# Graph attention and mean aggregation from neighbour lists: another order of the work where the adjacency ends and layer 0 begins, and biases folded on VectorE

## The chip, the cores and the metric

One core of a Trainium2 chip runs the whole kernel in one launch. The metric is the time on the device in microseconds. The kernel before takes 719.69 us, the median of 3 runs (718.86 to 720.13). The profile is of one execution with a span of 718.4 us.

## The reference

x is 4096 x 512, adj a 4096 x 4096 matrix of 0 and 1 with about four ones in a row. Two layers, each a graph layer with a residual and a layer norm:

```python
# layer 0: 8 heads of 64 columns
Wh = einsum('nf,hfo->hno', x, W)
f1 = einsum('hno,ho->hn', Wh, a[:, :64]); f2 = einsum('hno,ho->hn', Wh, a[:, 64:])
e = leaky_relu(f1[:, :, None] + f2[:, None, :], 0.2)
attn = softmax(where(adj > 0, e, -9e15), axis=-1)
x = layernorm(x + heads_side_by_side(attn @ Wh))
# layer 1
mask = (adj > 0); deg = mask.sum(1)
agg = mask @ x / maximum(deg, 1)
out = concat([x @ W_self + b_self, agg @ W_nb + b_nb]) @ W_comb + b_comb
x = layernorm(x + relu(out))
```

## The kernel before, in words

**Lists instead of masks.** Since a row of adj has few ones, the kernel turns every row into a list of column numbers and then gathers rows of a table in memory. The rows are worked on in 32 blocks of 128. A list has 3 places of its own (K0) and, for longer rows, shared places in two columns (KH) that one-hot matrices ("own", "st") tie to their rows. What doesn't fit sets a flag, and a dense program (`dense_layers`) runs; it doesn't run here.

**Stage 1, the lists** (lines 712 to 821). The loop over b has 30 turns (LB = 30), and blocks 30 and 31 come after it. For each block two loads of 1 MB bring the adjacency (`load_adj`, tile "at", 4 buffers, on SyncE's queue). ScalarE turns each half into bf16 (`mask_adj`, tile "ab", 3 buffers). TensorE packs the bits into keys (`fold_adj`, L395) and VectorE takes the greatest keys (`max_keys`, L410). Beside it `node_block` (L319) makes the rows of table t0, Wh with f2 in front, and stores them. Every four blocks a `decode` turns keys into column numbers; it's a generator, and each `some(lists)` runs one piece of it up to the next `yield`.

**The joint** (lines 812 to 858). The node rows of blocks 30 and 31 are finished; blocks 30 and 31 of the adjacency are loaded, masked, folded and decoded; the gathers of layer 0 for blocks 0 and 1 start (L515, GpSimd, five instructions of 128 rows for a block), those of later blocks once the pool of the adjacency ("lists") is closed. `fold_weights` (L259, L270) multiplies W_nb by the lower half of W_comb into m2, in four quarters, also as a generator. `fold_bias` (L279 to L289) turns b_nb into a column and multiplies it by the same half of W_comb: four products with one row of result, added to brow by VectorE.

**Stage 2, layer 0** (lines 864 to 902). Turn i works on several blocks at once: the layer norm of block i (`a_moments`, L611; `root`; `norm`), the weighted sum of block i+1 (L583, L595, L605, L607), the weights of block i+2 (`a_weights`, L539), and the product of block i-1 with m2 (`a_z`, L632), which is stored into table t1. Turns 2 to 7 also run one piece each of the last decode, that of blocks 28 to 31.

**Stage 3** (lines 903 to 924): W_self is multiplied by the upper half of W_comb into m1, its bias likewise, and `spread_bias` (L295) copies the summed bias row to all 128 partitions with a product by a row of ones. **Stage 4, layer 1** (lines 941 to 964): gathers from t1 (again 160 instructions), own rows times m1 (L656), sums, layer norm, store.

**What sets the order.** The program runs under `manual_schedule`: each engine works in the order of the text. The waits between the engines follow from the tiles: a tile taken from a pool with n buffers waits until the tile n before it in that pool has been read for the last time. The "own" tiles (4 buffers) serve both `decode` of early blocks and `owners`; PSUM tiles "sm", "pw", "nm" have 2 buffers, "key" has 1.

Of the kernel before, what the change touches and what calls it, by code (L numbers as in the profile page):

```python
# [40 lines left out]
P = 128  # L41
# [14 lines left out]
G = 4  # L56
# [30 lines left out]
def listed_layers(  # L87
# [112 lines left out]
    nc.vector.memset(onec, 1.0)  # L200
    eps = const.tile([P, 1], F32, name="eps")
    nc.vector.memset(eps, EPS)
    oner = const.tile([1, P], F32, name="oner")
    nc.vector.memset(oner, 1.0)
    inv_n = const.tile([P, 1], F32, name="inv_n")
    nc.scalar.mul(inv_n, onec, 1.0 / N)

# [39 lines left out]
    def load_bias(k):  # L247
        brw = small.tile([FB, P], F32, name="brw", bufs=1)
        nc.scalar.dma_start(brw, (b_self, b_nb)[k].rearrange("(c p) -> c p", p=P))
        return brw  # L250

    def fold_weights(loaded, m, wp, tag):

        wr, wc = loaded

        def turned(c):
            tp = ps.tile([P, FB, P], F32, name="sm", bufs=2)
            for d in range(FB):
                nc.tensor.transpose(tp[:, d, :], wr[:, c, ts(d, P)], ident)  # L259
            wT = wp.tile([P, FB, P], F32, name="xT", bufs=2)  # L260
            nc.scalar.copy(wT, tp)
            return wT

        wT = turned(0)
        for c in range(FB):
            nxt = turned(c + 1) if c + 1 < FB else None
            yield
            mp = ps.tile([P, HD], F32, name=tag, bufs=2)
            for d in range(FB):
                nc.tensor.matmul(  # L270
                    mp, lhsT=wT[:, d, :], rhs=wc[:, d, :], start=(d == 0), stop=(d == FB - 1)
                )
            nc.scalar.copy(m[:, c, :], mp)
            wT = nxt

    def fold_bias(loaded, brw):

        bt = ps.tile([P, FB], F32, name="sm", bufs=2)
        nc.tensor.transpose(bt, brw, ident[0:FB, 0:FB])  # L279
        bcol = small.tile([P, FB], F32, name="bcol", bufs=1)  # L280
        nc.scalar.copy(bcol, bt)
        yield
        bp = ps.tile([1, HD], F32, name="sm", bufs=2)
        for d in range(FB):
            nc.tensor.matmul(
                bp, lhsT=bcol[:, d : d + 1], rhs=loaded[1][:, d, :],
                start=(d == 0), stop=(d == FB - 1),
            )
        nc.vector.tensor_add(brow[0:1, :], bp, brow[0:1, :])  # L289
        yield  # L290

    def spread_bias():

        bp = ps.tile([P, HD], F32, name="sm", bufs=2)
        nc.tensor.matmul(bp, lhsT=oner, rhs=brow[0:1, :], start=True, stop=True)  # L295
        nc.scalar.copy(brow, bp)


# [64 lines left out]

    loads, masks, keys, kks = {}, {}, {}, {}

    def load_adj(b, ap, hs=range(NH)):

        for h in hs:
            at = loads[b, h] = ap.tile([P, NG // NH, SC], I32, name="at", bufs=4)
            r = b * P + h * (P // NH)  # L370
            nc.sync.dma_start(
                at, adj[r : r + P // NH, :].rearrange("(j r) (s c) -> (r s) j c", r=RG, s=SEG)
            )

    def mask_adj(b, h, ap):
        ab = masks[b, h] = ap.tile([P, NG // NH, SC], BF16, name="ab", bufs=3)
        nc.scalar.activation(  # L377
            ab, loads.pop((b, h)), AF.Relu, accum_out=asum[:, b, h : h + 1]
        )
# [32 lines left out]
    def decode(b0, dp, place, slow=False):  # L412
# [22 lines left out]
        for g in range(G):  # L435
            nc.vector.max(nb[:, g, 0:8], kj[:, g, :])
            nc.vector.match_replace(kj[:, g, :], nb[:, g, 0:8], kj[:, g, :], 0.0)
            nc.vector.max(nb[:, g, 8:16], kj[:, g, :])
        yield
        va = dp.tile([P, G, KL], F32, name="va", bufs=1)  # L440
        nc.vector.tensor_scalar(va, nb, float(SHIFT), None, OP.is_ge)
        nc.vector.tensor_reduce(deg[:, bs], va, AX.X, OP.add)
# [83 lines left out]
    def a_owners(b, wp):  # L526
        OWN[b] = owners(b, wp)
# [159 lines left out]
    def some(todo):  # L687
        for p in todo:
            next(p, None)
# [30 lines left out]
    pa = []  # L720
    for k in range(2):
        pa.append(ps.tile([P, HD], F32, name=("sm", "key")[k], bufs=(2, 1)[k]))
        nc.tensor.matmul(pa[k], lhsT=oner, rhs=av[0:1, k], start=True, stop=True)
    nc.scalar.copy(av[:, 0], pa[0])
    xT = transposed(0, wp)
    prs = fp.tile([P, FB, HD], F32, name="wc")
# [44 lines left out]
    def store(w, row, eng=nc.scalar):  # L771
        eng.dma_start(t0[2 + w * P : 2 + (w + 1) * P, :], row[:, 0:TW])
# [5 lines left out]
    for b in range(LB):  # L778
        for k in range(1 + (b == AHEAD)):
            load_x(w + k + XL)  # L780
            sum_x(w + k + XL, xacc)
        if b + 2 < LB:
            load_adj(b + 2, ap)
        elif b + 2 == LB:
            loaded = load_fold(1, w_nb, fp)
            load_adj(LB, ap, (0,))
        if b == 3:
            brw = load_bias(1)
            nc.scalar.dma_start(brow[0:1, :], b_comb.rearrange("(a o) -> a o", a=1))
            pads(wp)  # L790
        some(lists)
        nxt = transposed(w + 1, wp)
        if w > 0:
            store(w - 1, row)
        if b + 1 < LB:
            key_bank(b + 1)
            for h in range(NH):
                mask_adj(b + 1, h, ap)
            row = node_block(w, xT, b)
            w, xT = w + 1, nxt  # L800
        if b == AHEAD:
            nxt = transposed(w + 1, wp)
            store(w - 1, row)
            row = node_block(w, xT)
            w, xT = w + 1, nxt
        if b == 24:
            pieces = mean_row(w_sb, xacc, wp)
        if b >= 24:
            next(pieces, None)
        if b % G == G - 1:  # L810
            lists = [*lists[-1:], decode(b + 1 - G, dp, on_own)]
    row = node_block(w, xT)
    store(w, row)
    fold_adj(LB - 1, dp)
    max_keys(LB - 1)
    row = node_block(w + 1, nxt)
    store(w + 1, row, nc.sync)
    load_adj(LB, ap, (1,))
    load_adj(LB + 1, ap)
    xa_cm.__exit__(None, None, None)  # L820

# [2 lines left out]
    for b in range(2):  # L824
        G0[b] = gather(t0, b, gps)
    m2s = fold_weights(loaded, m2, wp, "pw")
    next(m2s)
    mask_adj(LB, 0, ap)
    some(lists)
    next(m2s)  # L830
    key_bank(LB)
    mask_adj(LB, 1, ap)
    some(lists)
    next(m2s)
    some(lists)
    fold_adj(LB, dp)
    max_keys(LB)
    a_owners(0, wp)
    a_owned(0, wp)
    mask_adj(LB + 1, 0, ap)  # L840
    next(m2s)
    key_bank(LB + 1)
    mask_adj(LB + 1, 1, ap)
    fold_adj(LB + 1, dp)
    max_keys(LB + 1)
    ap_cm.__exit__(None, None, None)
    gps += [ctx.enter_context(tc.tile_pool(name=f"gat{k}", bufs=1)) for k in range(2, GA)]
    sp_cm = tc.tile_pool(name="last", bufs=1, side="right")
    sp = sp_cm.__enter__()
    lists = [decode(NB - G, dp, on_last, slow=True)]  # L850
    some(lists)
    next(m2s, None)
    some(lists)
    for _ in fold_bias(loaded, brw):
        pass
    some(lists)
    m1_pool = ctx.enter_context(tc.tile_pool(name="m1", bufs=1))
    m1 = m1_pool.tile([P, FB, HD], F32, name="m1")
# [2 lines left out]
    def on(b):  # L861
        return 0 <= b < NB

    for i in range(-2, NB + 2):
# [5 lines left out]
            xT = transposed(i - 1, wp)  # L870
        if on(i + 1):
            a_reach(i + 1)
        if i >= -1 and on(i + 2):
            a_owned(i + 2, wp)
        if on(i + 1):
# [6 lines left out]
            root(i, xs[:, i, :])  # L882
        if on(i + 2):
            a_exp(i + 2)
        if on(i):
            norm(i, xs[:, i, :])
        if on(i - 1):
# [10 lines left out]
        if i == 1:  # L898
            loaded = load_fold(0, w_self, fp)
            brw = load_bias(0)  # L900
        if 2 <= i < 8:
            some(lists)
    for _ in fold_weights(loaded, m1, wp, "nm"):
        pass
    for _ in fold_bias(loaded, brw):
        pass
    spread_bias()


    sp_cm.__exit__(None, None, None)  # L910
# [446 lines left out]
```

## Time and profile before

| what | from the profile |
|---|---|
| span | 718.4 us, 9039 instructions |
| TensorE products, weight loads | 646.3 us (90%), 365.2 us (51%) |
| VectorE, ScalarE, GpSimd | 488.8 (68%), 443.7 (62%), 360.5 us (50%) |
| memory | 165.29 MB read, 25.31 MB written, 265 GB/s over the span |
| gathers L515 | 320, 951 ns each |
| masks L377 | 64, 1911 ns each |
| products of the weight fold L270 | 64 passes, 3.70 us for a quarter of 8 |

The page cuts the span into 40 slices and gives a digit for each engine, the busy share in tenths. They show that no engine sets the pace throughout, so a share of the whole span says little: one reads the stage that a change touches. In the time line each row is a group of like instructions of one engine with its start, length and, in brackets, the idle time of the engine before it and what ended that. L numbers are lines of the kernel before.

### The profile page before, as it was taken

The numbers are of one execution on the slowest core, as the hardware profiler recorded it, in microseconds if no ns is written. First come the engines' busy times: TensorE is split into PE (matmuls) and PEld (weight loads), VectorE is DVE, ScalarE is ACT, GpSimd is POOL, SyncE is SP. The second block draws the span as 40 slices with busy tenths as digits, with TensorE's granted clock in tenths as the row PEclk, the third lists the DMA queues.
The fourth block names the chain that finished last, engine by engine and source line by source line (L and its number), as shares of the span: only waits on it lengthen the run. The fifth ranks groups of instructions, "written<-read, shape, count | busy, mean of one in ns | idle before, by whom it ended". The sixth has DMA issues, their size and how long they took to land. (4 is left out here: it accounts for less than half of the span.)

```text
span 718.4 us, 9039 instructions
## 1 busy us (share of the span) xinstructions
PE 646.3 (90%) x2534; PEld 365.2 (51%) x2534; DVE 488.8 (68%) x1424; ACT 443.7 (62%) x915; POOL 360.5 (50%) x403
## 2 busy tenths in 40 slices
PE   4797888887999769999999999999999999999992
PEld 2465666655676335555555555554344444444440
DVE  5266777875876378999999999981116665566553
ACT  3567777676784315556666576664237777677764
POOL 6512222121002476566666666400777777777770
PEclk9989999999999978999999999999989999999997
DMA  9999999999997676977877887611667888888883
GB/s 282 389 352 394 393 393 394 393 391 392 390 391 265 216 211 204 316 213 206 231 228 231 232 227 230 185 44 45 200 203 245 258 254 260 254 258 258 262 255 108
DMA packets 84263, 191.28 MB, mean 266 GB/s; under 512 B 12513, under 2 KB 12521, under 8 KB 84206
## 3 DMA queue, kind: packets, MB, share of 16 engines
q0 software_dynamic: 25600, 84.56, 40.2%
q1 hardware_dynamic: 53952, 97.53, 37.0%
q10 hardware_dynamic: 4654, 8.54, 3.1%
q8 instruction: 22, 0.36, 0.2%
q14 instruction: 35, 0.29, 0.1%
HBM read 165.29 MB, written 25.31 MB: 265 GB/s over the span
## 5 line engine op out<-in xcount | busy, mean ns | idle before, releaser
L515 POOL DMA_INDIRECT g<-t,idx x320 | 304.4, 951 | 172.4 <-issue 120.2
L377 ACT ACTIVATE ab<-at 128x2048 bf16<-128x2048 int32 x64 | 122.3, 1911 | 55.8 <-DMA at<-in_adj_dram 49.6
L319 PE MATMUL pw<-w_sb,xT 128*128 128x264 f32 x512 | 133.4, 407 | 1.0 <-DVE row L323 0.9
L632 PE MATMUL pw<-m,xT 128*128 128x512 f32 x256 | 118.0, 604 | 3.1 <-ACT xT L313 1.7
L319 PEld LDWEIGHTS pw<-w_sb,xT 128*128 128x128 f32 x512 | 96.4, 198 | 29.3 <-issue 4.7
L313 ACT COPY xT<-tp 128x512 f32<-128x512 f32 x80 | 46.3, 579 | 91.5 <-PE tp L311 89.8
L305 POOL TENSOR_TENSOR xacc<-xacc,xs 128x512 f32<-128x512 f32 x32 | 41.1, 1284 | 122.6 <-DMA xs<-in_x_dram 122.0
L583 DVE TENSOR_TENSOR g<-g,key 128x1024 f32<-128x1024 f32 x64 | 77.9, 1217 | 1.1
L632 PEld LDWEIGHTS pw<-m,xT 128*128 128x128 f32 x256 | 46.1, 190 | 55.3 <-issue 45.8
L595 PE MATMUL nm<-g,own 128*128 128x512 f32 x128 | 66.3, 643 | 0.0
L656 PE MATMUL nm<-m,xT 128*128 128x512 f32 x128 | 60.4, 617 | 1.3 <-ACT xT L313 1.3
L311 PEld LDWEIGHTS tp<-ident,xs 128*128 128x128 f32 x320 | 40.9, 148 | 36.1 <-issue 29.8
L656 PE MATMUL pw<-m,xT 128*128 128x512 f32 x128 | 57.6, 593 | 0.0
L311 PE MATMUL tp<-ident,xs 128*128 128x128 f32 x320 | 50.6, 283 | 6.0 <-DMA xs<-in_x_dram 5.8
L323 DVE COPY row<-pw 128x264 f32<-128x264 f32 x64 | 27.1, 425 | 33.3 <-PE pw L319 23.9
L656 PEld LDWEIGHTS nm<-m,xT 128*128 128x128 f32 x128 | 24.1, 199 | 26.1 <-issue 24.6
L670 DVE SCALAR_TENSOR_TENSOR sm<-y,lst,nm 128x512 f32<-128x512 f32 x16 | 12.1, 755 | 36.7 <-PE nm L663 36.6
L670 DVE SCALAR_TENSOR_TENSOR sm<-y,lst,pw 128x512 f32<-128x512 f32 x16 | 12.1, 755 | 34.3 <-PE pw L663 34.3
L656 PEld LDWEIGHTS pw<-m,xT 128*128 128x128 f32 x128 | 23.2, 191 | 23.4 <-issue 23.4
L663 PE MATMUL pw<-g,own 128*128 128x512 f32 x64 | 31.4, 615 | 3.0 <-DMA g<-t,idx 3.0
L595 PEld LDWEIGHTS nm<-g,own 128*128 128x128 f32 x128 | 23.1, 200 | 16.9 <-issue 16.1
L549 PEld LDWEIGHTS sm<-e,own 128*128 128x128 f32 x128 | 19.8, 199 | 22.7 <-ACT e L543 11.6
(178 smaller groups left out, 1031.1 us busy)
## 6 DMA issues: line engine op xcount, KB each, us to landing
at<-in_adj_dram SPq DMA_DIRECT2D x64, 1024.0 KB, 11.2
t<-row SPq DMA_DIRECT2D x32, 256.0 KB, 3.6
out_dram<-row SPq DMA_DIRECT2D x32, 256.0 KB, 3.8
t<-row ACTq DMA_DIRECT2D x31, 260.0 KB, 6.0
xs<-in_x_dram SPq DMA_DIRECT2D x31, 256.0 KB, 11.5
g<-t,idx POOLq DMA_INDIRECT x320, 4.1
wc<-in_L_gnn_W_comb_dram SPq DMA_DIRECT2D x2, 1024.0 KB, 14.8
w_sb<-in_L_gnn_W_dram SPq DMA_DIRECT2D x8, 128.0 KB, 4.4
```

The costliest lines, as they stand in the source:

```text
L305: nc.gpsimd.tensor_tensor(xacc, xacc, xs[:, b, :], OP.add)
L311: nc.tensor.transpose(tp[:, c, :], xs[:, b, ts(c, P)], ident)
L313: nc.scalar.copy(t, tp)
L319: nc.tensor.matmul(pw, lhsT=xT[:, c, :], rhs=w_sb[:, c, k * HW : (k + 1) * HW], start=(c == 0), stop=(c == FB - 1),)
L323: nc.vector.tensor_copy(row[:, k * HW : (k + 1) * HW], pw)
L377: nc.scalar.activation(ab, loads.pop((b, h)), AF.Relu, accum_out=asum[:, b, h : h + 1])
L515: nc.gpsimd.indirect_dma_start(out=g[:, k, 0 : table.shape[1]], out_offset=None, in_=table[:, :], in_offset=bass.IndirectOffsetOnAxis(ap=i ...
L583: nc.vector.tensor_tensor(gv if to is None else to.rearrange("p (k h d) -> p k h d", k=1, h=H), gv, E[b][:, sl].unsqueeze(3).to_broadcast( ...
L595: nc.tensor.matmul(NM[b], lhsT=OWN[b][:, k, :], rhs=G0[b][:, K0 + k, H:TW], start=False, stop=(k == KH - 1), skip_group_check=True,)
L632: nc.tensor.matmul(pz, lhsT=xT[:, c, :], rhs=m2[:, c, :], start=(c == 0), stop=(c == FB - 1))
L656: nc.tensor.matmul(NM[b], lhsT=xT[:, c, :], rhs=m1[:, c, :], start=False, stop=False, skip_group_check=True,)
L663: nc.tensor.matmul(NM[b], lhsT=OWN[b][:, k, :], rhs=g[:, K0 + k, 0:HD], start=False, stop=(k == KH - 1), skip_group_check=True,)
```

## The change

It does these things:

- Block 30's second adjacency half is loaded with the first, at b = 28; only block 31 is loaded at the joint. Both halves of block 30 are masked before the last node block, and block 30 is folded before the weight product begins.
- `fold_weights` has a second `yield` after each quarter's product, so that the copy of a quarter can stand later than its product. Its pieces are spread anew: three quarters before layer 0, the last in turn i = -1.
- `a_owners(0)` stands before the last piece of decode(24).
- The last decode (`slow`) takes its maxima in four pieces. One piece runs before layer 0, one in turn -2, the others in turns 2 to 11.
- Biases: the bias column is made by `bias_column` (at b = 5 for W_nb, after layer 0 for W_self). `fold_bias` now multiplies the rows of W_comb by that column on VectorE, four instructions that add into brow, which is 128 partitions of partial sums. `sum_bias` adds these over the partitions and spreads the sum with one product by a 128 x 128 tile of ones, which takes the place of the row of ones.

It is meant to bring the last adjacency work and the start of layer 0 forward, and to take the one-row products off TensorE.

```diff
     eps = const.tile([P, 1], F32, name="eps")
     nc.vector.memset(eps, EPS)
-    oner = const.tile([1, P], F32, name="oner")
-    nc.vector.memset(oner, 1.0)
+    ones = const.tile([P, P], F32, name="ones")
+    nc.vector.memset(ones, 1.0)
     inv_n = const.tile([P, 1], F32, name="inv_n")
     nc.scalar.mul(inv_n, onec, 1.0 / N)
...
                     mp, lhsT=wT[:, d, :], rhs=wc[:, d, :], start=(d == 0), stop=(d == FB - 1)
                 )
+            yield
             nc.scalar.copy(m[:, c, :], mp)
             wT = nxt
-    def fold_bias(loaded, brw):
+    def bias_column(k, brw):
         bt = ps.tile([P, FB], F32, name="sm", bufs=2)
         nc.tensor.transpose(bt, brw, ident[0:FB, 0:FB])
-        bcol = small.tile([P, FB], F32, name="bcol", bufs=1)
+        bcol = small.tile([P, FB], F32, name=f"bcol{k}", bufs=1)
         nc.scalar.copy(bcol, bt)
-        yield
-        bp = ps.tile([1, HD], F32, name="sm", bufs=2)
+        return bcol
+
+    def fold_bias(loaded, bcol):
+
         for d in range(FB):
-            nc.tensor.matmul(
-                bp, lhsT=bcol[:, d : d + 1], rhs=loaded[1][:, d, :],
-                start=(d == 0), stop=(d == FB - 1),
-            )
-        nc.vector.tensor_add(brow[0:1, :], bp, brow[0:1, :])
-        yield
-
-    def spread_bias():
+            nc.vector.scalar_tensor_tensor(
+                brow, loaded[1][:, d, :], bcol[:, d : d + 1], brow, OP.mult, OP.add
+            )
+
+    def sum_bias():
         bp = ps.tile([P, HD], F32, name="sm", bufs=2)
-        nc.tensor.matmul(bp, lhsT=oner, rhs=brow[0:1, :], start=True, stop=True)
+        nc.tensor.matmul(bp, lhsT=ones, rhs=brow, start=True, stop=True)
         nc.scalar.copy(brow, bp)
...
     loads, masks, keys, kks = {}, {}, {}, {}
-    def load_adj(b, ap, hs=range(NH)):
-
-        for h in hs:
+    def load_adj(b, ap):
+
+        for h in range(NH):
             at = loads[b, h] = ap.tile([P, NG // NH, SC], I32, name="at", bufs=4)
             r = b * P + h * (P // NH)
...
             nc.vector.match_replace(kj[:, g, :], nb[:, g, 0:8], kj[:, g, :], 0.0)
             nc.vector.max(nb[:, g, 8:16], kj[:, g, :])
-        yield
+            if slow or g == G - 1:
+                yield
         va = dp.tile([P, G, KL], F32, name="va", bufs=1)
         nc.vector.tensor_scalar(va, nb, float(SHIFT), None, OP.is_ge)
...
     for k in range(2):
         pa.append(ps.tile([P, HD], F32, name=("sm", "key")[k], bufs=(2, 1)[k]))
-        nc.tensor.matmul(pa[k], lhsT=oner, rhs=av[0:1, k], start=True, stop=True)
+        nc.tensor.matmul(pa[k], lhsT=ones[0:1, :], rhs=av[0:1, k], start=True, stop=True)
     nc.scalar.copy(av[:, 0], pa[0])
     xT = transposed(0, wp)
...
         elif b + 2 == LB:
             loaded = load_fold(1, w_nb, fp)
-            load_adj(LB, ap, (0,))
+            load_adj(LB, ap)
         if b == 3:
             brw = load_bias(1)
+            nc.vector.memset(brow, 0.0)
             nc.scalar.dma_start(brow[0:1, :], b_comb.rearrange("(a o) -> a o", a=1))
             pads(wp)
...
             row = node_block(w, xT)
             w, xT = w + 1, nxt
+        if b == 5:
+            bcol = bias_column(1, brw)
         if b == 24:
             pieces = mean_row(w_sb, xacc, wp)
...
     row = node_block(w, xT)
     store(w, row)
+    key_bank(LB)
+    for h in range(NH):
+        mask_adj(LB, h, ap)
     fold_adj(LB - 1, dp)
     max_keys(LB - 1)
     row = node_block(w + 1, nxt)
     store(w + 1, row, nc.sync)
-    load_adj(LB, ap, (1,))
     load_adj(LB + 1, ap)
     xa_cm.__exit__(None, None, None)
...
         G0[b] = gather(t0, b, gps)
     m2s = fold_weights(loaded, m2, wp, "pw")
-    next(m2s)
-    mask_adj(LB, 0, ap)
-    some(lists)
-    next(m2s)
-    key_bank(LB)
-    mask_adj(LB, 1, ap)
-    some(lists)
-    next(m2s)
     some(lists)
     fold_adj(LB, dp)
     max_keys(LB)
-    a_owners(0, wp)
-    a_owned(0, wp)
-    mask_adj(LB + 1, 0, ap)
     next(m2s)
     key_bank(LB + 1)
+    some(lists)
+    for k in range(3):
+        next(m2s)
+    mask_adj(LB + 1, 0, ap)
+    a_owners(0, wp)
+    fold_bias(loaded, bcol)
+    some(lists)
     mask_adj(LB + 1, 1, ap)
+    next(m2s)
     fold_adj(LB + 1, dp)
     max_keys(LB + 1)
+    a_owned(0, wp)
+    next(m2s)
     ap_cm.__exit__(None, None, None)
     gps += [ctx.enter_context(tc.tile_pool(name=f"gat{k}", bufs=1)) for k in range(2, GA)]
...
     sp = sp_cm.__enter__()
     lists = [decode(NB - G, dp, on_last, slow=True)]
-    some(lists)
-    next(m2s, None)
-    some(lists)
-    for _ in fold_bias(loaded, brw):
-        pass
     some(lists)
     m1_pool = ctx.enter_context(tc.tile_pool(name="m1", bufs=1))
...
         if on(i + 1):
             a_reach(i + 1)
+        if i == -1:
+            next(m2s)
         if i >= -1 and on(i + 2):
             a_owned(i + 2, wp)
...
         if on(i + 2):
             a_exp(i + 2)
+        if i == -2:
+            next(m2s)
+            some(lists)
         if on(i):
             norm(i, xs[:, i, :])
...
             loaded = load_fold(0, w_self, fp)
             brw = load_bias(0)
-        if 2 <= i < 8:
+        if i == -1:
+            next(m2s, None)
+        if 2 <= i < 12:
             some(lists)
+    bcol = bias_column(0, brw)
+    fold_bias(loaded, bcol)
     for _ in fold_weights(loaded, m1, wp, "nm"):
         pass
-    for _ in fold_bias(loaded, brw):
-        pass
-    spread_bias()
+    sum_bias()
```

## The prediction

> **What bounds the kernel now.** I read the busy digits of the page first, to cut the span into stages, then the groups, then the time line around the joint that the diff edits.
>
> ```profile
> POOL 6512222121002476566666666400777777777770
> PEclk9989999999999978999999999999989999999997
> ...
> L515 POOL DMA_INDIRECT g<-t,idx x320 | 304.4, 951 | 172.4 <-issue 120.2
> ```
>
> A slice is 17.96 us. To slice 12 the adjacency streams in; slices 12 to 14 are the joint; to slice 26 runs layer 0; from slice 28 layer 1. L515 is every row gather; 160 belong to each layer. Idle time of GpSimd between the layers is one stretch of 41.6 us. Busy times of stretches (PE, PEld, DVE, ACT, POOL, then clock, DMA share, GB/s):
>
> ```profile
> 225.30:257.00 31.70, 24.28 (x84) 10.71 (x84) 15.49 (x65) 13.05 (x20) 17.04 (x18) 0.95 0.71 239
> 257.00:282.60 25.60, 19.79 (x60) 11.51 (x61) 19.92 (x53) 9.18 (x26) 16.99 (x18) 0.67 0.68 195
> 282.60:329.20 46.60, 43.91 (x179) 24.64 (x177) 43.07 (x115) 27.87 (x73) 28.72 (x31) 1.00 0.83 259
> 501.90:700.00 198.10, 195.44 (x551) 91.66 (x550) 100.68 (x222) 126.07 (x306) 149.97 (x159) 0.98 0.79 245
> ```
>
> Layer 1: 159 gathers start in 198.1 us, 1.246 us apiece, 0.95 of instruction and 0.30 of issue. The first starts at 501.88, the last at 701.19; 159 steps of 1.25 us make 198.8 of these 199.3 us. So layer 1 is a fixed length from its first gather, which waits for the last z rows in t1. **What counts is only when layer 0 ends.**
>
> Layer 0: the moments instruction L611 of blocks 0, 1, 2, 3, 8, 11 and 31 starts at 266.72, 275.38, 282.60, 290.98, 329.23, 349.63 and 488.57. Without decode work a block takes 6.80 us, VectorE without a gap; later 6.93 to 6.98, TensorE as the close second. From 282.6 to 329.2 VectorE has no gap to speak of, and what its last decode adds is paid in full: 46.63 - 6 x 6.80 = 5.83 us. So the joint, 225 to 283, can be shortened, and VectorE work put into blocks 2 to 10 comes back. The joint, in the time line:
>
> ```profile
> 225.28 1.55 SPq L371 DMA_DIRECT2D at<-in_adj_dram  x3
> ...
> 235.27 0.61 PE L395 MATMUL key<-ab,fold 128*32 128x512 bf16 x8
> ...
> 238.52 5.12 PE L270 MATMUL pw<-wc,xT 128*128 128x512 f32 x8
> ...
> 244.68 1.91 ACT L377 ACTIVATE ab<-at 128x2048 bf16<-128x2048 int32 x1
> ...
> 246.73 0.61 PE L395 MATMUL nm<-ab,fold 128*32 128x512 bf16 x6 [1.53 <-ACT ab L377]
> ...
> 247.45 0.89 DVE L410 MAX8 kk<-nm 128x8 f32<-128x128 f32 x4 [9.29 <-PE nm L395]
> ...
> 255.34 0.68 DVE L289 TENSOR_TENSOR brow<-sm,brow 1x512 f32<-1x512 f32 x1 [0.60 <-PE sm L285]
> ...
> 257.02 0.20 DVE L539 TENSOR_TENSOR e<-g,f1s 128x40 f32<-128x40 f32 x1
> ...
> 275.38 0.69 DVE L611 SCALAR_TENSOR_TENSOR y<-y,nm 128x512 f32<-128x512 f32 x1 [1.85 <-PE nm L595]
> ```
>
> Three of the four last loads are issued at 225.28, behind the store of the last row, while the memory is quiet (6 to 164 GB/s from 220 to 225). The last mask ends at 246.6, its fold at 247.34; VectorE has waited 9.29 us for it. Then VectorE runs decode(28): 3.0 us to the keys, 3.3 of maxima, the bias add, 1.0 of indices, and only at 257.02 the first weights of layer 0. At 275.38 it waits again, for products at half clock.
>
> **What the skill says.** The Trainium skill, "TensorE: Matmul & The Clock Gate", Part 1: the array falls to half rate after an idle window of about 3.4 us and needs about as long a busy one to recover. The trace agrees: after 2.23 us of idle in a thin stretch the clock is 0.50 from 238.4 to 241.7, and again from 258.8 to 275.6; the 8 passes of L270 take 5.12 instead of 3.70 us. The same page, "Architectural detail", says that ScalarE and VectorE are strict FIFO; that is why the order in the program decides below. "DMA: Bandwidth & Descriptors", "Queues, rings and completion order": within one ring descriptors are consumed in order. The trace: the SyncE loads of 1 MB land one after the other, 8.7 to 14.8 us after issue.
>
> **The change, part by part.**
>
> *Loads and masks of block 30.* Its second half is now issued right behind the first (210.94), when mask(28,1) has freed its buffer at 211.0: about 211.3. The first half landed 13.2 us after issue, at 224.1. One megabyte more is 2.7 us at 390 GB/s if it queues behind, 224.5 if it fills the free share after 220; I take 226.0. Masks: 224.2 to 226.2 and 226.3 to 228.2 (1.91 us each). fold(30) on TensorE, now ahead of the weight product, ends at 228.8 (0.61). TensorE, which went straight on at 224.19, thus idles some 3.9 us: a new wait, with the whole weight product queued behind it.
>
> *Weight product.* To the end of its second quarter: 8 transposes 1.04, the copy 0.3, product 3.70, 4 transposes 0.60, product 3.70 = 9.3 us, to 238.2. That idle gap is long enough for half clock; one stretch of 3.3 us at half rate costs 1.65: 239.8.
>
> *Decode(24) and the owners.* The tile "own" has four buffers, all held by decode(24), and a_owners(0) now comes before the products (L473, 16 in 1.86 us) that read them. VectorE must wait for the first four of these, 240.3; at worst for all, 241.7. Behind this wait stand owners 0.46, the four bias instructions, the rest of decode(24) 1.6, the maxima of block 31 0.9, and decode(28)'s keys 3.0. The bias form, 128x512 with two SBUF operands, isn't in the trace; bounds are half of L583's 1.22 for twice the elements (0.61) and L670's 0.755. I take 0.65, 2.6 for four. Sum: 240.3 + 0.46 + 2.6 + 1.6 + 0.9 + 3.0 = 248.9.
>
> *Last mask.* Two instead of three megabytes are issued at 225.3; together with 2.66 MB of gathers they moved to 242 at 390 GB/s, so they land some 2.7 us sooner, by 239. Masks of block 31 end by 241, fold(31) by 243; its maxima come at 245 on VectorE, so it is off the path. The gathers of blocks 2 to 4, which began at 248.09 behind fold(31), begin at about 244. Blocks 0 and 1 have landed.
>
> *Start of layer 0.* First weights at 249.0 instead of 257.02: 8.0 us earlier. The quarter of decode(28)'s maxima at i=-2 adds 0.8 (0.81 per group in the trace). The last quarter of the weight product stands in i=-1 ahead of a_owned(1), 3.7 us on TensorE beside 5.2 us on VectorE (1.22 + 0.4 + 3.3 and the small ones): hidden. Moments(0) 9.7 + 0.8 later: 259.5 instead of 266.72, 7.2 earlier. Blocks 0 to 2 take 15.88 us now, with 2.07 of waits for TensorE at half clock. In i=0 TensorE has only 3.4 us of work in 7, so I keep the 15.88.
>
> *Decode in the loop.* Three groups of maxima (2.43) and the indices (1.0) now fall into blocks 2 to 5, where VectorE has no gap: 3.4 back. The loop ends its decode three blocks later, so 20 instead of 23 blocks run at TensorE's pitch: 3 x 0.15, 0.4 gained.
>
> *At no cost.* The memset of brow and bias_column(1) (0.22 and 0.17) lie in the stage that loads the adjacency at 390 GB/s; the pads' memset already made ScalarE's queue wait for VectorE there. bias_column(0), four bias instructions on an idle VectorE and one product replace 6.3 us of chain between 514.2 and 520.5, hidden by 30 gathers (37.5 us) of lead. The ones tile changes nothing.
>
> Sum: -8.0 + 0.8 + 3.4 - 0.4 = -4.2: 719.7 - 4.2 = **715.5 us**.
>
> **Rivals.**
>
> *TensorE stays warm* (22%). For it: from 243.6 to 247 it was thinly busy at full clock. Against it: 258.8 to 275.6. The joint is 1.65 us shorter and blocks 0 to 2 lose their 2.07: 711.8.
>
> *The gain is given back* (14%). The late landing (226.8), the wait for all 16 products (1.4) and bias instructions of 0.755 (0.4) put the first weights at 251.6, and the product at i=-1 delays block 0 by 1 us more: -5.4 + 1.0 + 0.8 + 3.4 - 0.4 = -0.6: 719.1.
>
> *A wait in place of the one removed* (14%, slower). TensorE's idle behind the masks lasts longer (second half at 228, as under the full load of 14.8 us from a later issue, +2) and the 11 us of weight product and decode products run at half clock not for one window but for three (+3.3 more). With the rival above, first weights come near 256: -1 + 0.8 + 1 + 3.4 - 0.4 = +3.8, less 2 if blocks 0 to 2 warm up: 721.5. For it: half clock lasted 16.8 us once. Against it: then TensorE was less than half busy, and here it's dense.
>
> **Numbers.** Forecast 50%, rivals 22, 14, 14. The forecast and the first rival are faster; the third is half within 0.2% (1.44 us). Faster 0.76, same 0.10, slower 0.14. The range from 711.3, below the warm case, to 719.8, above the given-back case, leaves out the slower rival and a little below.
>
> **What would show it.** Right: mask(30,1) ends near 228 and TensorE idles before fold(30); the first gather of block 2 near 244; first weights near 249; moments(2) near 275.5; blocks 2 to 10 about 3.4 us longer than the decode blocks before; the first layer-1 gather near 497.7 and 198.8 us from there to the last. Wrong, if the first weights come after 253, if an engine other than VectorE sets blocks 2 to 10, if the first gathers come later than 228, or if GpSimd gets gaps in layer 1.

## The result, and the profile after

The changed kernel takes 716.92 us (median of 7 executions, 715.71 to 718.42), the kernel before beside it 719.69 us (median of 7, 718.46 to 721.61). The ratio is 0.9957, with a 95% interval of 0.994 to 0.9975. Two later comparisons, on two chips, gave 0.9968 (0.9954 to 0.9982) and 0.996 (0.9947 to 0.9974). So the change is faster by some 2.3 to 3.1 us; 715.5 us was forecast.

The profile of the changed kernel, span 714.0 us, is of the fastest of its seven executions (715.71 us), that of the kernel before of one at 720.06 us; so the profiled difference of 4.4 us is larger than that of the medians. The page shows the slices of GpSimd, the granted clock, and the gathers:

```profile
POOL 6512122221101677666666666400777777777771
PEclk9989999999998989999999999999999999999995
...
L516 POOL DMA_INDIRECT g<-t,idx x320 | 304.7, 952 | 168.6 <-issue 79.0
```

Line numbers after L515 are one higher than before. The gathers cost what they did, and in layer 1 they are still the bound: from the first (498.72) to the last start (697.70) 198.98 us, against 199.31 before. The first one starts 3.16 us sooner than before; that is the part of the gain that can be followed step by step. The rest of the profiled difference is 0.3 us in the gathers and 0.9 us after the last one, where profiles of the same kernel differ by as much.

Busy times of four stretches (PE, PEld, DVE, ACT, POOL, then clock, DMA share, GB/s): the joint, turns -2 to 1, blocks 2 to 8, layer 1.

```profile
225.30:249.87 24.57, 18.10 (x75) 9.67 (x74) 13.72 (x47) 10.93 (x16) 14.37 (x15) 0.86 0.74 237
249.87:276.33 26.46, 21.04 (x72) 11.58 (x72) 20.55 (x58) 10.19 (x29) 19.91 (x22) 0.87 0.75 208
276.33:323.01 46.68, 43.14 (x164) 23.06 (x164) 43.52 (x124) 27.88 (x74) 29.74 (x31) 1.00 0.84 265
498.70:697.70 199.00, 192.50 (x546) 90.68 (x545) 103.34 (x226) 129.86 (x313) 150.54 (x159) 0.99 0.81 247
```

Before, the joint lasted to 257.02. It's 7.15 us shorter, but the clock in it has dropped from 0.95 to 0.86; turns -2 to 1 behind it take about as long as before (26.46 against 25.58 us) at a clock of 0.87 instead of 0.67. The time line of the changed kernel, in order:

```profile
224.27 1.91 ACT L377 ACTIVATE ab<-at 128x2048 bf16<-128x2048 int32 x1 [2.55 <-DMA at<-in_adj_dram]
...
226.32 0.39 PE L395 MATMUL key<-ab,fold 128*32 128x512 bf16 x2 [1.99 <-ACT ab L377]
...
227.53 1.91 ACT L377 ACTIVATE ab<-at 128x2048 bf16<-128x2048 int32 x1 [1.26 <-DMA at<-in_adj_dram]
...
229.58 1.04 PE L395 MATMUL key<-ab,fold 128*32 128x512 bf16 x6 [2.87 <-ACT ab L377]
...
230.72 0.89 DVE L410 MAX8 kk<-key 128x8 f32<-128x128 f32 x4 [4.68 <-PE key L395]
...
232.38 4.44 PE L270 MATMUL pw<-wc,xT 128*128 128x512 f32 x8
...
240.53 1.86 PE L474 MATMUL sm<-lst,own 128*128 128x24 f32 x16
...
241.09 0.63 DVE L508 TENSOR_SCALAR own<-iota,es 128x128 f32<-128x128 f32 x2 [4.33 <-PE sm L474]
241.49 3.11 DVE L288 SCALAR_TENSOR_TENSOR brow<-wc,bcol,brow 128x512 f32<-128x512 f32 x4
...
242.80 0.61 PE L395 MATMUL nm<-ab,fold 128*32 128x512 bf16 x8
...
246.02 0.89 DVE L410 MAX8 kk<-nm 128x8 f32<-128x128 f32 x4
...
249.87 0.19 DVE L540 TENSOR_TENSOR e<-g,f1s 128x40 f32<-128x40 f32 x1
...
250.62 0.71 PE L550 MATMUL sm<-e,own 128*128 128x8 f32 x4 [3.14 <-ACT e L544]
...
252.70 6.22 PE L270 MATMUL pw<-wc,xT 128*128 128x512 f32 x8
...
259.17 0.37 ACT L535 COPY st<-sm 128x256 f32<-128x256 f32 x1 [8.13 <-PE sm L533]
...
260.23 0.18 DVE L559 TENSOR_REDUCE dn<-e 128x8 f32<-128x24 f32 x1 [2.38 <-ACT e L544]
...
262.72 0.69 DVE L612 SCALAR_TENSOR_TENSOR y<-y,nm 128x512 f32<-128x512 f32 x1 [1.07 <-PE nm L596]
```

The wait of 9.29 us for the last fold is gone: its maxima at 246.02 wait for nothing. In its place stand a wait of TensorE for the masks of block 30 (2.87 us, and 1.99 ahead of it) and one of VectorE for the product L474 (4.33 us). The four bias instructions at 241.49 take 3.11 us of VectorE; before, the bias cost VectorE 0.68 us at 255.34 and a wait of 0.60, so by the two time lines this part of the change, where it stands, adds some 1.8 us to VectorE's work ahead of the first weights. At 252.70 the last quarter of the weight product takes 6.22 us; ScalarE, which has to copy the transposes behind it, waits 8.13 us and holds up the exponent of block 1 and with it VectorE.

Starts of the moments (before L611, after L612), first weights and first gather of layer 1, in us:

| | weights 0 | moments 0 | 2 | 11 | 31 | gather |
|---|---|---|---|---|---|---|
| before | 257.02 | 266.72 | 282.60 | 349.63 | 488.57 | 501.88 |
| after | 249.87 | 262.72 | 276.33 | 346.95 | 485.18 | 498.72 |
| gain | 7.15 | 4.00 | 6.27 | 2.68 | 3.39 | 3.16 |

### The profile page after: what moved, and what is told of

Read it like the earlier page. It is cut to its first block, busy times and chain, and to the rows that moved or that the text cites. A ratio compares the mean times of both kernels' runs of the same rounds, so it can differ in the third digit from the quotient of the medians.

```text
span 714.0 us, 9013 instructions
## 1 busy us (share of the span) xinstructions
PE 635.5 (89%) x2518; PEld 359.0 (50%) x2518; DVE 495.0 (69%) x1431; ACT 444.9 (62%) x915; POOL 360.6 (51%) x403
## 4 chain that ended last, share of the span: by engine, by line
PE 59%; DMA 15%; DVE 13%; issue 6%; ACT 4%; SPq 1%; POOL 1%; ACTq 0%; POOLq 0%; DVEq 0%
PE pw L633 11%; DMA at<-in_adj_dram 10%; PE nm L657 7%; PE pw L657 7%; PE pw L319 7%; PE nm L596 5%; PE pw L664 4%; PE nm L664 3%; DMA g<-t,idx 3%; PE tp L311 3%; PE nm L270 2%; PE pw L270 2%; ACT xT L313 2%; DMA xs<-in_x_dram 2%; DVE g L584 2%
## 5 line engine op out<-in xcount | busy, mean ns | idle before, releaser
L319 PE MATMUL pw<-w_sb,xT 128*128 128x264 f32 x512 | 131.7, 403 | 1.3 <-DVE row L323 1.2
L596 PE MATMUL nm<-g,own 128*128 128x512 f32 x128 | 62.7, 612 | 0.0
L657 PE MATMUL nm<-m,xT 128*128 128x512 f32 x128 | 57.7, 593 | 1.5 <-ACT xT L313 1.5
L664 PE MATMUL nm<-g,own 128*128 128x512 f32 x64 | 31.8, 621 | 4.7 <-DMA g<-t,idx 4.7
L647 DVE TENSOR_TENSOR sm<-sm,g 128x512 f32<-128x512 f32 x32 | 22.2, 695 | 19.7 <-ACT sm L643 19.5
```

The lines of the kernel that those rows point to most:

```text
L319: nc.tensor.matmul(pw, lhsT=xT[:, c, :], rhs=w_sb[:, c, k * HW : (k + 1) * HW], start=(c == 0), stop=(c == FB - 1),)
L596: nc.tensor.matmul(NM[b], lhsT=OWN[b][:, k, :], rhs=G0[b][:, K0 + k, H:TW], start=False, stop=(k == KH - 1), skip_group_check=True,)
L657: nc.tensor.matmul(NM[b], lhsT=xT[:, c, :], rhs=m1[:, c, :], start=False, stop=False, skip_group_check=True,)
L664: nc.tensor.matmul(NM[b], lhsT=OWN[b][:, k, :], rhs=g[:, K0 + k, 0:HD], start=False, stop=(k == KH - 1), skip_group_check=True,)
```

## The clock runs in windows

The first finding decides how all the other runs are read. The Trainium skill, "TensorE: Matmul & The Clock Gate", Part 1, "What's actually happening", says that the activity window is 4096 cycles, 3413 ns, and that it is "free-running". Below, half clock stands for a granted clock of 0.50. Cutting the profile into stretches of half a microsecond gives the length of each stretch at half clock. In the 14 profiles of this study, from 150 to 330 us, 44 such stretches lie whole. Each is 3.41, 6.83, 10.24, 13.66 or 17.07 us long within 0.01, and all starts in one profile lie on one grid of 3.413 us. So the trace agrees, and a profile can be cut on its own grid. The changed kernel (TensorE's busy time, granted clock, DMA share, GB/s):

```profile
223.69:227.10 3.41, 1.04 (x5) 1.00 0.41 137
227.10:230.51 3.41, 0.93 (x6) 0.50 0.99 351
230.51:233.93 3.42, 3.42 (x13) 0.50 1.04 396
...
247.58:250.99 3.41, 0.37 (x4) 1.00 0.73 200
250.99:254.41 3.42, 2.93 (x9) 0.50 0.75 202
254.41:257.82 3.41, 3.41 (x5) 0.50 0.72 212
257.82:261.23 3.41, 2.29 (x10) 1.00 0.72 205
```

Around the joint the clock of a window can be read from the window before it. In the nine profiles cut in this way (those of the table below), from some 220 to 283 us, every window with at most 1.80 us of busy TensorE is followed by one at half clock, and no window at full clock with 1.88 us or more is; at 1.86 us it went both ways. This isn't a rule for the whole program: in the kernel before, the windows from 94.81 and 122.11 had 1.80 and 1.64 us, and full clock followed. Once at half clock, a fully busy window brought full clock back, with one exception in the kernel before; of those with 2.9 to 3.4 us one did (3.14) and seven didn't (up to 3.36). From 150 us on two more of these did (3.17 and 3.39). So which amount is enough stays open, but work that starts again in the middle of a window at half clock mostly stayed slow to the end of the next, fully busy one. TensorE was idle here for 1.99 and 2.87 us, with a fold of 0.39 us between them, and paid two windows.

## Experiments

All kernels below start from the changed one unless the text says otherwise. The table has every interval that is used (us): "mask" is the start of the last mask of block 30, w0 the first weights, m2 and m11 the moments of blocks 2 and 11. The last column is the time at half clock from 222 to 286.

| kernel | mask to L474 | L474 to w0 | w0 to m2 | m2 to m11 | half clock |
|---|---|---|---|---|---|
| before | - | - | 25.58 | 67.03 | 20.5 |
| changed | 13.00 | 9.34 | 26.46 | 70.62 | 13.7 |
| changed, again | 12.95 | 9.34 | 27.05 | 70.57 | 17.1 |
| changed, third | 13.70 | 9.34 | 28.66 | 70.62 | 20.5 |
| biases early | 12.80 | 7.19 | 25.81 | 70.67 | 13.7 |
| biases early, again | 13.83 | 7.19 | 24.47 | 70.69 | 10.2 |
| quarter early | 13.53 | 9.34 | 24.51 | 70.59 | 17.1 |
| both early | 12.41 | 7.19 | 26.88 | 70.63 | 17.1 |
| biases early, TensorE filled | 11.34 | 7.19 | 28.64 | 70.61 | 13.7 |

In these profiles, and for a given order of the work, L474 to w0 is the same to 0.01 us and m2 to m11 to 0.12 us: VectorE sets them. The other two differ by up to 1.0 and 2.2 us between executions of one kernel: TensorE and its windows set those.

### Control

The changed kernel, unedited, beside three of the runs below.

> The changed kernel once more, beside the three that follow. Both theories: 0.9957 of the time before within its interval, some 716.9 us. If the joint's order decides, its first weights of layer 0 come near 249.9 us again and its block 0 near 262.7; if the phase of TensorE's clock decides, these move by 1 to 3 us between executions of one program.

717.66 us (median of 22), before 719.91 (35): 0.9968 (0.9954 to 0.9982). The moments of block 2 came at 277.89 instead of 276.33: the last adjacency landed 1 us later, and one more window at half clock fell at 268.97.

### The biases in a wait that is there anyway

The 3.11 us of bias work on VectorE stand behind the wait for L474. Some 15 us earlier VectorE waits 4.68 us for the fold of block 30.

```diff
     some(lists)
+    fold_bias(loaded, bcol)
     fold_adj(LB, dp)
...
     a_owners(0, wp)
-    fold_bias(loaded, bcol)
     some(lists)
```

> The four bias instructions (3.11 us) move up, ahead of the maxima of block 30, where VectorE idles for 4.68 us. Theory 1, VectorE's chain sets the start of layer 0: the owners still wait for L474, the rest of the decode waits for its last product at 242.4 instead of for the bias at 244.5, so the first weights come 2.0 us sooner (247.9) and the kernel takes 2.0 us less, about 714.9. Theory 2, TensorE's weight product sets the start: the third quarter still ends at 247.5, at most 0.5 us is gained.

712.33 us, ratio 0.99 (0.9869 to 0.993). The time line of this kernel:

```profile
225.76 3.10 DVE L288 SCALAR_TENSOR_TENSOR brow<-wc,bcol,brow 128x512 f32<-128x512 f32 x4
...
240.75 0.48 DVE L508 TENSOR_SCALAR own<-iota,es 128x128 f32<-128x128 f32 x2 [4.13 <-PE sm L474]
...
242.09 0.29 DVE L478 COPY es<-sm 128x128 f32<-128x128 f32 x1 [0.86 <-PE sm L474]
...
247.38 0.19 DVE L540 TENSOR_TENSOR e<-g,f1s 128x40 f32<-128x40 f32 x1
...
248.13 0.61 PE L550 MATMUL sm<-e,own 128*128 128x8 f32 x4 [1.25 <-ACT e L544]
...
249.80 5.38 PE L270 MATMUL pw<-wc,xT 128*128 128x512 f32 x8
```

From L474 to the first weights it's 7.19 us instead of 9.34. The gain is 2.15 of the 3.11 us; 0.86 us become a wait for the second half of L474. The whole kernel gained more, 4.9 us by the ratios, (0.9968 - 0.99) x 719.9. TensorE waits only 1.25 us ahead of L550, where the changed kernel waited 3.14: with less work of VectorE between them, the turn before the last quarter is less empty. Here one window at half clock followed, not two. In the profiles the moments of block 2 come 4.70 us sooner than in the control: 2.15 us here, 1.25 between w0 and m2, and 1.16 because the last adjacency landed sooner (mask at 227.39 instead of 228.55). In the repetition below it's 6.24 us, of which 4.20 lie between w0 and m2. That this part comes from the windows is a reading of these traces, and no edit shows it by itself.

### The last quarter out of turn -1

The quarter goes behind the third one, before layer 0, and the third one's copy with it; its own copy stays at the end of turn -1.

```diff
-    next(m2s)
+    for k in range(3):
+        next(m2s)
     ap_cm.__exit__(None, None, None)
...
-        if i == -1:
-            next(m2s)
...
-            next(m2s)
             some(lists)
```

> The last quarter of the weight product moves out of turn -1 to right behind the third, where TensorE idles from 247.5 to 250.6. Theory 1, the quarter at half clock (6.22 us) ahead of a_owned(1) holds up block 0: from first weights to moments(0) 10.4 instead of 12.9 us, the kernel takes about 2.4 us less, 714.5. Theory 2, the clock is the limit whatever the place: the products of turns -1 and 0 then run at half clock as in the kernel before, moments(0) to moments(2) takes 15.9 instead of 13.6 us and nothing is gained.

715.1 us, ratio 0.9932 (0.9913 to 0.9951). First weights to moments of block 0: 8.80 us instead of 12.85. Without the quarter the next turns are empty, though, and from there to the moments of block 2 it took 15.71 us instead of 13.61. So the quarter did delay block 0 by some 4 us. That it also keeps the clock up afterwards isn't shown: in the third profile of the changed kernel the turns behind the quarter took 15.50 us, with two windows at half clock.

> Both edits. Theory 1: they lie one behind the other on VectorE's chain, so the gains add up but for the half microsecond by which the two quarters on TensorE now reach past the first weights: about 4 us less than the changed kernel, 713. Theory 2: no less than the better of the two alone.

Both edits together: 713.64 us, 0.9913 (0.9883 to 0.9943), no better than the biases alone. TensorE's windows in this kernel:

```profile
249.33:252.74 3.41, 1.46 (x11) 1.00 0.71 212
252.74:256.16 3.42, 2.92 (x7) 0.50 0.76 213
256.16:259.57 3.41, 2.90 (x9) 0.50 0.70 206
259.57:262.98 3.41, 1.07 (x5) 0.50 0.76 221
262.98:266.40 3.42, 3.42 (x5) 0.50 0.72 213
```

Four windows in a row stay at half clock, and none before the last is full. The gains don't add: 4.9 us for the biases and 2.6 for the quarter, by the ratios, make 4.0 together. The 713 us that were expected came out only because the biases alone had gained more than twice the 2.0 us expected of them.

### On a slower chip: decode, load, idle time

The next four ran on a chip where the kernel before takes 787.51 us, so only ratios and stages up to the first weights are compared. The changed kernel was not run there. In all four profiles an engine stands still in turn -1 or 0, from 3 to 8 us after the product that it waits for has ended, and nothing in the profile releases it; no profile of the other chips shows this between 225 and 290 us.

The decode as one piece ahead of layer 0, as before the change:

```diff
-            if slow or g == G - 1:
+            if g == G - 1:
...
-    some(lists)
+    for _ in range(3):
+        some(lists)
...
-        if 2 <= i < 12:
+        if 2 <= i < 8:
```

(and the piece in turn -2 goes)

> The changed kernel with the last decode as before: its maxima (3.3 us) and its indices (1.0) whole, ahead of layer 0, four turns of the loop fewer with a piece. Theory 1, VectorE has no gap in blocks 2 to 10, so a piece costs the same there as ahead of the loop: the first weights come 4.3 us later, blocks 2 to 11 take 67.0 instead of 70.6 us, the kernel stays within 1 us of 717. Theory 2, the pieces are hidden in the loop and dividing them is the gain: about 3.5 us more, 720.5.

781.12 us, 0.9923 (0.9886 to 0.9959). L474 to first weights: 13.73 us, 4.4 more than the 9.34 with the decode spread. Moments of block 2 to 11: 68.47 us, against 72.2 to 72.4 in the three other runs of that chip, 3.8 less. The piece that left turn -2 is another 0.8 us of VectorE's work there (estimate from the 0.81 us of a group of maxima in the kernel before). So what the spread decode saves in the joint it gives back whole: of the 7.15 us by which the changed kernel's first weights come sooner, some 4.4 are decode work put off, not saved.

Block 30's second half loaded late, and its mask behind it:

```diff
-            load_adj(LB, ap)
+            load_adj(LB, ap, (0,))
...
-    for h in range(NH):
-        mask_adj(LB, h, ap)
+    mask_adj(LB, 0, ap)
...
-    load_adj(LB + 1, ap)
+    load_adj(LB, ap, (1,))
+    load_adj(LB + 1, ap)
+    mask_adj(LB, 1, ap)
```

> The changed kernel with the second half of block 30 loaded behind the store of the last row, as before; the order of the rest is kept. Theory 1, the load must come early for this order to work: the half lands near 232 instead of 227.5, TensorE stands before fold(30) until 235, the first weights come 4 to 5 us later (254 to 255), the kernel takes about 5 us more, 721 to 722. Theory 2, the load is hidden and only the order of the engines counts: first weights within 1 us of 250 to 251.

A single execution, 789.37 us. The second mask starts behind its load:

```profile
231.13 1.91 ACT L377 ACTIVATE ab<-at 128x2048 bf16<-128x2048 int32 x1 [4.76 <-DMA at<-in_adj_dram]
```

L474 starts at 243.80: 3.3 us later than in the changed kernel, and 4.0 later than in the run with the whole decode on the same chip (239.76). The first weights come at 253.14, 3.3 us later too, where 4 to 5 were expected. The early load is needed by the new order.

32 transposes that nothing reads, ahead of the fold of block 30, fill TensorE's idle time:

```diff
     some(lists)
+    warm = ps.tile([P, FB, P], F32, name="tp", bufs=1)
+    for _ in range(8):
+        for d in range(FB):
+            nc.tensor.transpose(warm[:, d, :], xs[:, NB - 1, ts(d, P)], ident)
     fold_adj(LB, dp)
```

> The changed kernel with 32 transposes whose result nobody reads ahead of fold(30), 4.3 us of work for TensorE while it waits for the two masks. Theory 1, the wait puts TensorE at half clock and that is on the path: the clock stays at 1.00 from 227 to 234, eight transposes take 1.04 instead of 1.97 us and the first quarter 3.7 instead of 4.4, the products L474 come 1.9 us sooner after the second mask, and so do the first weights: about 715. Theory 2, VectorE's own work sets the start: no change, 717.

779.69 us, 0.9898 (0.9868 to 0.9928). The rows of TensorE that took 1.04 and 4.44 us take 0.61 and 3.68 here, and L474 follows:

```profile
229.89 0.61 PE L395 MATMUL key<-ab,fold 128*32 128x512 bf16 x6 [1.41 <-ACT ab L377]
...
231.79 3.68 PE L270 MATMUL pw<-wc,xT 128*128 128x512 f32 x8
...
239.18 1.86 PE L474 MATMUL sm<-lst,own 128*128 128x24 f32 x16
```

From the last mask to L474 it's 11.34 us instead of 13.0, and instead of 12.48 in the run with the whole decode on this chip, which has one window at half clock there. So half clock there cost the changed kernel some 1.6 us. The first weights gained less: L474 to w0 is 9.69 us, as L478 stood 0.35 us after the bias work.

The same with both early edits, and more unread transposes in turns -1 and 0 (`busy(n)` stands for n of them):

```diff
     some(lists)
     fold_bias(loaded, bcol)
+    busy(32)
     fold_adj(LB, dp)
...
+        if i in (-1, 0):
+            busy((12, 20)[i + 1])
```

> Bias and last quarter moved as before (the fourth kernel of the first comparison), with unread transposes on TensorE in three places: 32 ahead of fold(30), 12 in turn -1, 20 in turn 0. Theory 1, half clock ate the gain of the moved quarter: moments(0) to moments(2) takes 13.6 instead of 15.6 us, first weights to moments(0) 9.5 instead of 11.3, the first weights come 1.9 sooner: about 5 us less than without, 709. Theory 2, the transposes stand in the way of what they should speed up: no gain or a loss of up to 2 us, 713 to 716.

779.84 us, 0.9895 (0.9862 to 0.9928): mask to L474 11.33 us again, and no more gained behind it; the 5 us more that were expected didn't come. Here the standing still can be seen twice on VectorE:

```profile
242.54 0.29 DVE L478 COPY es<-sm 128x128 f32<-128x128 f32 x1 [3.35 <-remote]
...
258.36 0.17 DVE L559 TENSOR_REDUCE dn<-e 128x8 f32<-128x24 f32 x1
...
264.57 0.16 DVE L562 TENSOR_TENSOR dn<-dn,sm 128x8 f32<-128x8 f32 x1 [6.04 <-remote]
...
264.89 0.94 POOL L516 DMA_INDIRECT g<-t,idx  x1 [3.01 <-DVE dn L562]
```

The product that L478 waits for had ended 2.6 us earlier, so that L474 to w0 is 9.69 us and not the 7.19 of the early biases. The product that L562 waits for had ended 8 us earlier, and the other engines soon stand with it. In the three other runs of this chip ScalarE's copy L535 stood in the same way, from 3.0 us (whole decode) over 6.2 (the run before) to 7.8 us (late load) after its transposes had ended. The cause stays open. It hides what the transposes in turns -1 and 0 are worth, and it makes the whole times of this chip a weak witness for any of the four edits.

### Again on another chip: the control, the biases, the best edits together, and the load alone

> The changed kernel as it is, run beside the two below and the kernel before, so that all four can be compared on one chip. All theories: ratio to the kernel before 0.994 to 0.998; where the profile has no stretch in which all engines stand, the weight product at about 241, the first weights of layer 0 at 250, the moments of block 2 at 276 to 278.

718.24 us (20 executions), before 720.73 (39): 0.996 (0.9947 to 0.9974).

> The sum of the biases put into VectorE's wait ahead of the fold of block 30, as in the earlier run. Theory (the wait for TensorE hides the 3.1 us): L474 to the first weights 7.2 us instead of 9.3, ratio 0.990 (0.987 to 0.993), some 5 us less than the changed kernel beside it, of which only 2.2 us can be the four instructions and the rest is a shorter turn 0 and -1. Rival (the earlier run was lucky by its DMA timing): ratio within 0.002 of the changed kernel's beside it, with the 2.2 us lost again between the first weights and the moments of block 2.

714.1 us, 0.9901 (0.9873 to 0.993): as the first time. The rival, luck by the timing of the DMA, falls, since it was the same on another chip. But the two profiles differ where the same program has the same idle times. Of the second:

```profile
246.24:249.65 3.41, 2.22 (x6) 1.00 0.58 155
249.65:253.06 3.41, 2.73 (x12) 1.00 0.75 190
253.06:256.48 3.42, 2.31 (x8) 1.00 0.79 219
```

and of the first:

```profile
247.04:250.45 3.41, 1.70 (x10) 1.00 0.68 198
250.45:253.87 3.42, 3.42 (x6) 0.50 0.74 215
253.87:257.28 3.41, 2.29 (x10) 1.00 0.74 216
```

The grid cuts the same two gaps (1.25 and 0.62 us) in two ways. In the one, no window is below 2.22 us and the last quarter takes 3.68 us; in the other, one window has 1.70 and the quarter takes 5.38 us. First weights to the moments of block 0 take 9.90 us in the one and 11.59 in the other.

Biases early, and the 32 transposes behind them:

```diff
     some(lists)
+    fold_bias(loaded, bcol)
+    warm = ps.tile([P, FB, P], F32, name="tp", bufs=1)
+    for _ in range(8):
+        for d in range(FB):
+            nc.tensor.transpose(warm[:, d, :], xs[:, NB - 1, ts(d, P)], ident)
     fold_adj(LB, dp)
```

> The sum of the biases in VectorE's wait, and 32 unread transposes on TensorE ahead of the fold of block 30 (they fill its two waits for the masks and keep the clock up). Theory (both gains lie on the chain through the weight product, one after the other): from the last mask to L474 11.3 us instead of 12.8, L474 to the first weights 7.2 us, so the moments of block 2 some 1.6 us sooner than with the biases alone, and the end 1.5 us sooner: ratio 0.988. Rival (the gathers or the owed weight product set the pace by then): the first weights 1.6 us sooner but the moments of block 2 or of block 11 at the same time as with the biases alone, ratio equal to it within 0.001.

711.71 us, 0.9865 (0.9835 to 0.9895), the fastest of all: clearly faster than both kernels beside it (changed 0.996). Against the biases alone (0.9901) the intervals overlap. Its profile has the expected 11.34 and 7.19 us, the first weights at 246.30. There two windows at half clock fell on the last quarter, and the moments of block 2 came at 274.94, 1.5 us later than with the biases alone (273.43). So the gain ahead of the first weights is shown, and that it reaches the end rests on the times, not on this profile, which is of the slowest of its four executions (713.39).

The kernel before, with the early load and nothing else:

```diff
-            load_adj(LB, ap, (0,))
+            load_adj(LB, ap)
...
-    load_adj(LB, ap, (1,))
     load_adj(LB + 1, ap)
```

> The kernel before with one part of the change alone: both halves of the last adj block asked for in the loop, none after it; masks, folds, decode and weight product in the old order. Theory (in the old order the second mask of block 30 starts behind VectorE's other work at 230.75, not behind its load, and the folds of the last block wait for TensorE): the first weights at 257 as before, within 0.7 us, ratio 0.998 to 1.002. Rival (the load set the old order's mask too): the mask 1.5 to 3 us sooner, the first weights with it, ratio 0.996 or less.

720.74 us against 720.73: 0.9999 (0.9984 to 1.0013). In the old order the load was hidden; it pays only with the masks brought forward. In its profile, of the slowest of its 20 executions, the first weights came at 261.36, not within 0.7 us of 257: the masks already stood 1.3 us later, and two windows at half clock fell on the last quarter, which took 6.26 us instead of 3.70. The expectation of a place in one profile missed; that of the time held.

## Why the prediction was right, and which step failed

*Loads and masks of block 30: right, mis-sized.* The second mask was to start at 226.3 and started at 227.53, just behind its load: later than the 226.8 of the second rival, sooner than the 228 of the third. TensorE idled for 4.9 us there, not 3.9.

*Half clock behind the masks: mis-sized.* The prediction took an idle window of about 3.4 us from the page that it cites and said that the trace agrees; but its own figure, 2.23 us of idle time, is shorter, and the measurements above decide: a window that is busy in part was enough. "One stretch of 3.3 us at half rate costs 1.65" was two windows, 6.83 us. It cost 1.6 us all the same, by the filled kernel, because for half of the 6.83 us TensorE had little to do. L474 came at 240.53, 0.7 later than the 239.8 forecast.

*Bias work: mis-sized.* Four instructions took 3.11 us, 0.78 each, where 0.65 was taken and the upper bound was 0.755. The first weights came at 249.87 (forecast 249.0). The first part of the sum, -8.0, was -7.15.

*The last quarter in turn -1: the step that failed.* "3.7 us on TensorE beside 5.2 us on VectorE: hidden." It took 6.22 us, to 258.92. VectorE's work did run beside it, but ended at 257.85, and then VectorE waited 2.38 us more: behind the quarter in TensorE's queue stand the transposes of a_owned(1), behind these ScalarE's copy, and behind this in ScalarE's order the exponent on which VectorE waits. First weights to the first moments took 12.85 us, not 10.5. With the quarter gone it was 8.80; with the quarter at full clock (biases early, again) 9.90. So about 1 us of the delay is its place in the order, and about 3 us is the clock, as far as two profiles of different orders show it. The step that failed is thus the full clock that was taken for the quarter, behind a turn that leaves TensorE nearly empty.

*Blocks 0 to 2: "I keep the 15.88" was 13.61.* This is the second half of the rival that TensorE stays warm (2.07 us): from 257.82 to 330 no window was at half clock, where before there were 17 us of it. Both errors nearly cancel, so that the moments of block 2 came at 276.33, where the sums give 275.4. That is luck of this execution: in the two repetitions of the changed kernel blocks 0 to 2 took 14.22 and 15.50 us, as more windows fell at half clock, and the moments of block 2 came at 277.89 and 279.67.

*Decode in the loop: right.* Forecast 3.4 back; blocks 2 to 11 take 70.6 instead of 67.03 us, 3.6, the same in the eight profiles of the table that have the new order. The whole decode gave 3.8 on its own. Later blocks gave 0.7, forecast 0.4.

*Layer 1: right.* 198.98 us from first to last gather. The edits that were costed at nothing there (bias column, bias sum, ones tile) show no effect: GpSimd has no gap in it and the first gather follows the last moments by 13.54 us, 13.31 before. That they cost nothing was read from the profile, and not tried by itself.

*The rivals.* "A wait in place of the one removed" was near in its two parts, with a mask at 227.53 and two windows at half clock where it had 228 and three, and wrong about what they cost: the slower case doesn't come out of them. "Given back" has the right place, turn -1, with some 2.4 us over the forecast instead of 1.

*The signs.* One of the signs of being wrong came: the first gathers start at 229.04, later than 228. It was ill-chosen, since they start at 228.04 in the kernel before, and no engine waits for them in the joint: the first weights at 249.87 follow VectorE's own work.

## What to carry to other kernels

Filling a wait of VectorE with work that has to be done anyway was worth more than the reorder itself: look, before moving work ahead of a critical wait, whether an earlier wait on the same engine can hold it. Work that is put "beside" other work on a shared queue should be costed by what is queued behind it, engine by engine, until one comes back to the engine that sets the pace. Where TensorE is thinly used, sum its busy time over windows of 3.413 us, at the worst position of the grid: in the three profiles of the changed kernel, one and two half-clock windows more went with 0.6 and 2.2 us more from the first weights to the moments of block 2.

## What was not expected of the hardware

Half clock came only in whole windows of 3.413 us, on a grid whose phase differs from profile to profile (44 stretches in 14 profiles). No long idle time was needed for it: 1.7 us of work in a window was too little here, and gaps of 1.25 and 0.62 us were enough where both lay in one window. The interval from the last mask to L474 was 11.34, 12.41 and 12.8 to 13.83 us with none, one and two such windows. Over the 20 executions of the changed kernel in the last comparison the mean clock ran from 0.956 to 0.974, and the longer spans had the lower clock (correlation -0.78; -0.57 over the 22 of the control). Over the 35 and 39 executions of the kernel before, beside these, there is no such relation (-0.01 and -0.04), so the windows are not the only thing that makes its times differ.
